# Graph attention on one core: which edge groups make their keys and values from node rows, when, and by what way the rows come

## The chip, the cores and the metric

The kernel runs on one core of a Trainium2 chip. The time is device microseconds of one launch; the figure for the kernel before is the median of three runs. One execution was profiled and gives the trace that is read here. All data start and end in the chip's memory (DRAM below).

## The reference, cut to what matters

There are 3125 nodes with 128 features each (`x`), 100,000 edges sorted by their target `dst`, five relations (`edge_type`), and eight heads of 16 features.

```python
for r in range(5):
    mask = edge_type == r
    q = einsum('eh,khd->ekd', x[dst], W_Q[r])
    k = einsum('eh,khd->ekd', x[src], W_K[r])
    v = einsum('eh,khd->ekd', x[src], W_V[r])
    logits = where(mask, (q * k).sum(-1) / 4 + bias[r], -1e9)
    top = maximum(segment_max(logits, dst), -1e9)
    e = where(mask, exp(logits - top[dst]), 0)
    attn = e / (segment_sum(e, dst)[dst] + 1e-12)
    out += segment_sum(attn[:, :, None] * v, dst)
h = out @ out_w.T + out_b + x
x1 = layernorm(h) * gamma + beta
result = layernorm(x + x1)
```

An edge has one relation, so it needs one key and one value row: those of its source node under its own relation.

## The kernel before, in words

**Table stage (0 to about 110 us).** The nodes are cut into `NT` = 25 blocks of 128. For each block `b`, `turn(b)` transposes the node rows and `table(b)` makes keys and values of all five relations in three fp32 matmuls (L404); ACT and DVE copy them out of PSUM (L408 and beside it) and SP's queue stores 640 KB to `kv_d` in DRAM. Row `node * 5 + relation` of `kv_d` is then 256 fp32: key and value. Beside each block stand jobs of the dictionary `side` (indices, keys and types of the edges are turned and converted), and from `b` = 1 on a gather `in_row` (L435) with an ACT `sign` that counts edges below a node (`count`, L443), eight gathers ahead.

**Loop.** Edges come in `NGR` = 196 groups of 512 (128 partitions x `T` = 4). A hand-written order walks over steps `k`; nothing is rescheduled, so each engine and each queue runs its instructions in the order in which the code issues them. Group `g` has its first half in step `g` and its second half (`v`) 16 to 19 steps later, when the maxima of its node block are there. In a step are issued, in this order:

- SP's queue: `fetch_keys` and `fetch_q` for group `k + 3`, rows of later stages, `fetch_types`, and further down the step `store_logits`.
- POOL: `gather` for group `k + 3`: four indirect DMAs (L699), one for each of the four columns of 128 edges, from `kv_d` into `kvs_[g % 23]`. There are `KVB` = 23 such buffers; the last reader of a buffer is `weigh` (L939). Then, about every eighth step, `maxima_load` (L830, tile `ell`): an indirect DMA that reads back logits stored in the step before.
- ACT: `put_kv` (L791), then `by_node`, `carry` (L988).
- PE: `spread_m` (L921, tile `me`), `sums` (L973, L975, L982), `spread_q` (L804, tile `qe`).
- DVE and ACT: `weigh` (L939), `less_max` (L930), `exps` (L934), `weights` (L947), `norm` (L994), `logits` (L817, L818), `spot` (L795, tile `hot`, made for group `k + 2` and kept in `HELD` buffers until `spread_m` of that group has read it), `places` (L959, L962), and around every eighth step in two steps `maxima` (L868 `wl`, L874 `mx`).
- End of the step: per node block `project`, `roots`, `norms`, and the queries of later blocks (L725).

**The x groups.** For the groups in `XG` (before: 3, 6, 9, 12, 15), `gather` does nothing. Instead the node rows themselves are gathered before the table stage: 20 indirect DMAs (L655) straight into the value half of `kvs_[g]`, with index `src` (tile `xi`), which need no table. Keys and values are then made in the loop, in steps `x_at[g] = step_of[g] - 5` and the two after it:

- `turn_x` (L764): four transposes of the rows into PSUM tile `tx`;
- `by_relation` (L771): for each relation, one DVE instruction that multiplies the rows by `type == r` (tile `xm`, 128 x 2560). `tr` holds the types of the 512 edges on every partition, fetched by `fetch_types` two steps before from `edge_type` as int32 (256 KB);
- `products` (L782), in the step after: twice ten products of 128 x 256, summed over the relations in tile `pk`; an fp32 product has two passes in the trace, so a group has 40;
- `put_kv` (L791), at the head of the step after that: two ACT copies into `kvs_[g]`.

PSUM tiles `tx`, `pk` and `me` carry one tag with two banks: each waits until the reader of the tile before the last is done. `xm` shares its memory with the maxima's `wl` (tag `wl`, one buffer).

Of the kernel before, what the change touches and what calls it, by code (L numbers as in the profile page):

```python
# [8 lines left out]
F32 = mybir.dt.float32  # L9
BF16 = mybir.dt.bfloat16  # L10
I32 = mybir.dt.int32
# [6 lines left out]
P = 128  # L18
# [3 lines left out]
R = 5  # L22
HEADS = 8
HD = 16
H = 128
# [14 lines left out]
GE = 512  # L40
T = GE // P
NGR = -(-E // GE)
HG = 99
HR = NGR - HG
# [14 lines left out]
NSR = E // SR  # L59
SB = P * E // N // SR  # L60
SPAD = 5
XG = range(3, 16, 3)
QB = 3
KVB = 23
HELD = 21
KVA = 9


# [65 lines left out]
def windowed_path(  # L134
# [4 lines left out]
    nc = tc.nc  # L139
# [6 lines left out]
    m_d = dram.tile([NP * R, 3 * HEADS], BF16, name="m_d")  # L146
    lg_d = dram.tile([GP, LW], F32, name="lg_d")
    key_d = dram.tile([NGR, GE], BF16, name="key_d")


    def keep(name, shape, dt=F32):
# [19 lines left out]
    xi = keep("xi", [P, len(XG), T], I32)  # L171

    kvs_ = {}

    def buffers(those):
        for i in those:
# [2 lines left out]
            )  # L179


    at_once = [*(g for g in range(5) if g not in XG), *XG]
    buffers(at_once)
    ahead = ctx.enter_context(tc.tile_pool(name="ahead", bufs=3))

# [7 lines left out]
    xn = load.tile([P, NT, H], F32, name="xn")  # L193
    nc.vector.memset(xn[:, NT - 1, :], 0.0)
    nc.sync.dma_start(xn[:, :4, :], x[: 4 * P].rearrange("(i p) h -> p i h", p=P))
    nc.sync.dma_start(
        xi,
        src[: (NGR - 1) * GE].rearrange("(g p t) -> p g t", p=P, t=T)[
            :, XG.start : XG.stop : XG.step, :
        ],  # L200
    )
    fr = load.tile([1, NGR + NSR], I32, name="fr")
    with nc.allow_non_contiguous_dma(reason="one element of each group"):
        nc.sync.dma_start(
# [257 lines left out]
    def keys_b():  # L462
# [4 lines left out]
        for p0, p1 in ((0, HR - 1), (HR - 1, HR)):  # L467
            nc.scalar.dma_start(
                key_d[HG + p0 : HG + p1, :], keyb[p0:p1, 1].rearrange("g t p -> g (t p)")
            )  # L470

    def keys_c():
        nc.vector.scalar_tensor_tensor(
            kvrow.rearrange("g s i -> g (s i)"), src_r.rearrange("g s i -> g (s i)"), float(R),
            typ_r.rearrange("g s i -> g (s i)"), op0=ALU.mult, op1=ALU.add,
        )
        nc.scalar.activation(typr, typ_r, AF.Identity, bias=1.0)
# [150 lines left out]
    def no_maxima():  # L628
# [18 lines left out]
        13: [lambda: along(typr, 1, put_typ)],  # L647
        14: [no_maxima],
        15: [sorted_rows],
        17: [sorted_ends],  # L650
    }

    for i, g in enumerate(XG):
        for t in range(T):
            nc.gpsimd.indirect_dma_start(  # L655
                out=kvs_[g][:, t, H:], out_offset=None, in_=x[:, :],
                in_offset=bass.IndirectOffsetOnAxis(ap=xi[:, i, t : t + 1], axis=0),
            )
    rows, counted = {}, 0
    xT = {b: turn(b) for b in range(2)}  # L660
    for b in range(NT):
        if b + 2 < NT:
            xT[b + 2] = turn(b + 2)
        table(b, xT.pop(b))
        for f in side.get(b, ()):
            f()
        while b >= 1 and len(rows) < NT and len(rows) - counted < 8:
            rows[len(rows)] = in_row(len(rows))
        if b >= 3:
            count(counted, rows[counted])  # L670
            counted += 1
# [81 lines left out]


    def fetch_types(g):
        tr = ahead.tile([P, GE], I32, name="tr", bufs=1)
        nc.sync.dma_start(tr, edge_type[g * GE : (g + 1) * GE].partition_broadcast(P))
        live["tr", g] = tr

    def turn_x(g):  # L760
        xe = kvs_[g % KVB][:, :, H:]
        tx = ps.tile([P, T, P], F32, name="tx", tag="me")
        for t in range(T):
            nc.tensor.transpose(tx[:, t, :], xe[:, t, :], ident)  # L764
        live["tx", g] = tx

    def by_relation(g):
        tr, tx = live.pop(("tr", g)), live.pop(("tx", g))
        xm = late_flow.tile([P, R, T, P], F32, name="xm", tag="wl", bufs=1)
        for r in range(R):  # L770
            nc.vector.scalar_tensor_tensor(  # L771
                xm[:, r], tr.rearrange("h (p t) -> h t p", t=T), float(r), tx,
                op0=ALU.is_equal, op1=ALU.mult,
            )
        live["xm", g] = xm
# [267 lines left out]
    def norms(b):  # L1043
        sd, mv = live.pop(("sd", b)), live.pop(("mv", b))
        nc.vector.reciprocal(sd, sd)
        if b < NT:
            n = min(P, N - b * P)
            h = live.pop(("h", b))
            nc.vector.scalar_tensor_tensor(
                h[:n], h[:n], mv[:n, 0, 0:1], gamma_t[:n], op0=ALU.subtract, op1=ALU.mult  # L1050
            )
            y = late_flow.tile([P, H], F32, name="y")
            nc.vector.scalar_tensor_tensor(
                y[:n], h[:n], sd[:n, 0:1], live.pop(("xr", b))[:n], op0=ALU.mult, op1=ALU.add
            )
            if ("mv", b + 1) not in live:
                live["mv", b + 1] = pair()
                nc.vector.memset(live["mv", b + 1], 0.0)
            nxt = live["mv", b + 1]
            moments(nxt[:, 1, :], y[:n], n)  # L1060
            live["y", b] = y
        if b:
            n = min(P, N - (b - 1) * P)
            z = late_flow.tile([P, H], F32, name="z")
            nc.vector.tensor_scalar(
                z[:n], live.pop(("y", b - 1))[:n], mv[:n, 1, 0:1], sd[:n, 1:2],
                op0=ALU.subtract, op1=ALU.mult,
            )
            live["z", b - 1] = z
# [36 lines left out]
    norm_at = {b: r + (r < final - 1) for b, r in root_at.items()}  # L1106


    x_at = {g: step_of[g] - 5 for g in XG}
    assert min(x_at.values()) >= -2 and max(x_at.values()) + 2 < at_k[0] - 1  # L1110


    q_from = []
# [10 lines left out]
    for k in range(-4, root_at[NT] + 2):  # L1124
# [20 lines left out]
                fetch_m(u)  # L1145
        for u in XG:
            if x_at[u] - 2 == k:
                fetch_types(u)

        while gathered < NGR - 1 and step_of[gathered + 1] <= k + (AHEAD if k < final - 16 else 1):  # L1150
# [585 lines left out]
```

## Time and profile before

| | |
|---|---|
| runs | 1665.2 us median (1658.07 to 1668.21) |
| profiled execution | time 1665.2 us, span 1663.5 us |
| mean granted TensorE clock | 0.724 |
| busy share of the span | PE 63%, DVE 57%, POOL 48%, ACT 38% |
| table stage, x gathers at the start | L655, 20 gathers from 11.8 us on, 0.944 us each |
| gathers in the loop | L699, 764, 0.948 us each |
| products of the x groups | L782, 200 records, 62.9 us busy |
| masks of the x groups | L771, 25, about 1.055 us each |

The span runs from the first to the last instruction of the profiled execution; the time of a run holds a little more around it. A busy share is the mean over all stages. In the trace PE's matmuls and its weight loads (PEld) are told apart; a "pass" below is one matmul record. Idle time is put down to what released the engine; "issue" is idle time with no such cause in the records.

### The profile page before, as it was taken

The numbers are of one execution on the slowest core, as the hardware profiler recorded it, in microseconds if no ns is written. First come the engines' busy times: TensorE is split into PE (matmuls) and PEld (weight loads), VectorE is DVE, ScalarE is ACT, GpSimd is POOL, SyncE is SP. The second block draws the span as 40 slices with busy tenths as digits, with TensorE's granted clock in tenths as the row PEclk, the third lists the DMA queues.
The fourth block names the chain that finished last, engine by engine and source line by source line (L and its number), as shares of the span: only waits on it lengthen the run. The fifth ranks groups of instructions, "written<-read, shape, count | busy, mean of one in ns | idle before, by whom it ended". The sixth has DMA issues, their size and how long they took to land.

```text
span 1663.5 us, 26129 instructions
## 1 busy us (share of the span) xinstructions
PE 1043.0 (63%) x7746; PEld 790.5 (48%) x7746; DVE 945.4 (57%) x2536; ACT 638.7 (38%) x2258; POOL 796.5 (48%) x901
## 2 busy tenths in 40 slices
PE   6774836356566666665666666666566655665676
PEld 2443624245454444554554554555445544454564
DVE  3452626455564665556466555657555564564686
ACT  1450103144344444434445443444344343334344
POOL 6345061645465545545645554555455455445400
PEclk8885967677676767667676766777666776666878
DMA  6683343445455544544545454555445444444400
GB/s 161 232 309 105 72 134 80 108 124 137 101 135 126 132 110 121 137 109 118 144 118 129 126 137 107 137 131 131 108 120 139 109 122 120 107 118 108 102 16 15
DMA packets 181946, 203.66 MB, mean 122 GB/s; under 512 B 83943, under 2 KB 146819, under 8 KB 181676
## 3 DMA queue, kind: packets, MB, share of 16 engines
q0 software_dynamic: 40576, 112.08, 23.4%
q1 hardware_dynamic: 136790, 85.12, 21.9%
q10 hardware_dynamic: 4430, 4.71, 1.1%
q8 instruction: 64, 1.05, 0.3%
q14 instruction: 86, 0.70, 0.1%
HBM read 166.51 MB, written 35.28 MB: 121 GB/s over the span
## 4 chain that ended last, share of the span: by engine, by line
PE 29%; DVE 28%; issue 19%; another core or an unknown queue 10%; ACT 5%; DMA 2%; SPq 1%; DVEq 0%; ACTq 0%; POOL 0%
PE pp L973 9%; PE qe L804 4%; PE me L921 4%; DVE wl L868 4%; DVE mx L874 4%; DVE prod L817 4%; PE pk L782 3%; DVE wv L939 3%; DVE lg L818 2%; PE pp L975 2%; PE pr L404 2%; ACT at L959 2%; DVE hot L795 2%; PE prq L725 1%
## 5 line engine op out<-in xcount | busy, mean ns | idle before, releaser
L699 POOL DMA_INDIRECT kv<-kv_d,idx x764 | 724.5, 948 | 587.9 <-DVE den L994 346.6
L973 PE MATMUL pp<-wv,at 128*125 128x136 f32 x1568 | 392.7, 385 | 43.3 <-issue 34.1
L973 PEld LDWEIGHTS pp<-wv,at 128*125 128x125 f32 x1568 | 295.7, 256 | 122.4 <-issue 116.0
L804 PE MATMUL qe<-qw,hot 125*128 125x128 bf16 x2352 | 229.9, 256 | 87.7 <-issue 77.6
L921 PE MATMUL me<-mw,hot 125*128 125x64 bf16 (+1 forms) x2352 | 145.3, 217 | 217.6 <-issue 115.2
L804 PEld LDWEIGHTS <-hot 125*128 125x128 bf16 x2352 | 203.3, 125 | 99.6 <-issue 86.3
L921 PEld LDWEIGHTS <-hot 125*128 125x128 bf16 x2352 | 126.6, 113 | 253.5 <-issue 197.0
L934 ACT ACTIVATE me<-me 128x32 f32<-128x32 f32 x196 | 35.7, 182 | 542.0 <-DVE me L930 409.5
L959 ACT ACTIVATE at<-row_at,nkey 128x125 f32<-128x125 f32 x744 | 237.6, 398 | 0.0
L930 DVE TENSOR_TENSOR me<-lg,me 128x32 f32<-128x32 f32 x196 | 37.7, 193 | 348.6 <-remote 195.6
L939 DVE TENSOR_TENSOR wv<-kv,me 128x512 f32<-128x512 f32 x196 | 133.0, 679 | 104.0 <-remote 63.2
L817 DVE TENSOR_TENSOR prod<-kv,qe 128x512 f32<-128x512 f32 x196 | 132.9, 678 | 43.2 <-PE qe L804 25.7
L818 DVE TENSOR_REDUCE lg<-prod 128x32 f32<-128x512 f32 x196 | 134.5, 686 | 6.8
L975 PE MATMUL pp<-pt,carried 125*5 125x136 f32 x390 | 101.4, 350 | 57.8 <-ACT pt L988 27.4
L962 ACT ACTIVATE at<-at 128x500 f32<-128x500 f32 (+1 forms) x196 | 117.3, 599 | 6.2
L725 PE MATMUL prq<-wq,xTq 128*128 128x384 f32 (+1 forms) x88 | 52.7, 693 | 92.9 <-DVE hot L795 61.1
L1007 ACT COPY oT<-pp 128x25 f32 x196 | 33.7, 172 | 180.6 <-PE me L921 72.8
L830 POOL DMA_INDIRECT ell<-lg_d,start_i x25 | 23.6, 944 | 154.3 <-DMA lg_d<-lg 62.0
L782 PE MATMUL pk<-wkv,xm 128*128 128x256 f32 x200 | 62.9, 448 | 50.3 <-issue 46.3
L868 DVE TENSOR_TENSOR wl<-by_head,shut 128x1536 f32<-128x1536 f32 (+2 forms) x49 | 73.1, 1491 | 33.7 <-PE pk L782 25.6
L982 PEld LDWEIGHTS pp<-rsum,o 125*128 125x128 f32 x392 | 83.6, 257 | 14.0 <-issue 13.3
L982 PE MATMUL pp<-rsum,o 125*128 125x25 f32 x392 | 74.2, 270 | 12.8 <-issue 8.2
(191 smaller groups left out, 1199.5 us busy)
## 6 DMA issues: line engine op xcount, KB each, us to landing
kt<-key_d SPq DMA_DIRECT2D x196, 128.0 KB
qw<-q_d SPq DMA_DIRECT2D x196, 96.0 KB
kv_d<-kvs SPq DMA_DIRECT2D x24, 640.0 KB
kv<-kv_d,idx POOLq DMA_INDIRECT x764
q_d<-q SPq DMA_DIRECT2D x22, 480.0 KB
lg_d<-lg SPq DMA_DIRECT2D x196, 18.0 KB
mw<-m_d SPq DMA_DIRECT2D x196, 6.0 KB
xr<-in_x SPq DMA_DIRECT2D x24, 64.0 KB
```

The costliest lines, as they stand in the source:

```text
L699: nc.gpsimd.indirect_dma_start(out=kv[:, t, :], out_offset=None, in_=kv_d[:, :], in_offset=bass.IndirectOffsetOnAxis(ap=idx[:, t, g : g + ...
L804: nc.tensor.matmul(qe[:, t, :], hot[:, t, :], qw[:WR, s, :], start=(s == 0), stop=(s == 2))
L817: nc.vector.tensor_tensor(prod, kv[:, :, :H], live.pop(("qe", g)), op=ALU.mult)
L818: nc.vector.tensor_reduce(lg[:, :, :HEADS], prod.rearrange("p t (k d) -> p t k d", d=HD), AX.X, ALU.add)
L868: nc.vector.tensor_tensor(wl, by_head[:, None].to_broadcast([P, n, nh, D]), shut[:, :n, None, :].to_broadcast([P, n, nh, D]), op=ALU.add,)
L921: nc.tensor.matmul(me[:, t], hot[:, t, :], mw[:WR, None, :, s, :].to_broadcast([WR, times, 2, HEADS // 2]), start=(s == 0), stop=(s == 2),)
L939: nc.vector.tensor_tensor(wv[:, :, :H].rearrange("p t (k d) -> p t k d", d=HD), kv[:, :, H:].rearrange("p t (k d) -> p t k d", d=HD), live ...
L959: nc.scalar.activation(at[:, t, :], row_at[:, :WR], AF.Abs, bias=nkey[:, t, g : g + 1], scale=1.0)
L962: nc.scalar.activation(at[:, on_dve:], at[:, on_dve:], AF.Relu, bias=1.0, scale=-1.0)
L973: nc.tensor.matmul(pp, at[:, t, :], wv[:, t, :], start=(t == 0), stop=(t == T - 1))
L975: nc.tensor.matmul(pp[:R], carried[:WR, g, :], live.pop(("pt", g - 1)), start=False, stop=False,)
L982: nc.tensor.matmul(op, live.pop(("o5", done)), rsum[:WR], start=True, stop=True)
```

## The change

- `XG` becomes 3, 8, 13, 18, 23, 44, 60, 76, 92: nine groups. The loop has 748 gathers (L699) instead of 764.
- The node rows no longer go to the value half of a group's buffer. They are gathered into tile `xs` with four buffers (`XA`): 16 gathers stand at POOL's head before the table stage, and 20 more follow one by one in the iterations `b` = 3 to 22, before that iteration's `count`. `store_x` writes each finished group (256 KB) to `xs_d` in DRAM, on SP's queue, at `b` = 3, 4, 5, 6, 8, 12, 16, 20 and 24. In the loop `fetch_nodes` brings it back into tile `xe` (one buffer).
- The types are converted once to bf16 and put in order (`types_d`, at `b` = 16: one DVE copy and three DMAs issued by ACT) and stored to `typ_d`; `fetch_types` reads 128 KB of bf16 from there, and `by_relation` reads them without a stride.
- `x_at` becomes `step_of[g] - 3`: transposes and masks in step `g - 3`, products in `g - 2`, copies at the head of `g - 1`; both fetches in step `g - 5`.
- `xm` has memory of its own. `HELD` goes from 21 to 20, and `z`, the last result of a node block, has one buffer instead of two.
- The groups whose gathers stand ahead of the loop's other memory (`at_once`) are 0, 1, 2, 4, 5, 6 and 7.

On POOL's queue 11 groups (44 gathers) now stand ahead of the first `ell`, then 7 groups (28) ahead of the second and 7 ahead of the third; before, 9 (36), 8 (32) and 8 (32).

```diff
--- before.py
+++ after.py
@@ -59,10 +59,12 @@
 NSR = E // SR
 SB = P * E // N // SR
 SPAD = 5
-XG = range(3, 16, 3)
+XG = (*range(3, 24, 5), *range(44, 93, 16))
+XE = 5
+XA = 4
 QB = 3
 KVB = 23
-HELD = 21
+HELD = 20
 KVA = 9
 
 
@@ -146,6 +148,8 @@
     m_d = dram.tile([NP * R, 3 * HEADS], BF16, name="m_d")
     lg_d = dram.tile([GP, LW], F32, name="lg_d")
     key_d = dram.tile([NGR, GE], BF16, name="key_d")
+    typ_d = dram.tile([NGR, GE], BF16, name="typ_d")
+    xs_d = dram.tile([len(XG) * P, T * H], F32, name="xs_d")
 
 
     def keep(name, shape, dt=F32):
@@ -179,7 +183,7 @@
             )
 
 
-    at_once = [*(g for g in range(5) if g not in XG), *XG]
+    at_once = [g for g in range(KVA - 1) if g not in XG]
     buffers(at_once)
     ahead = ctx.enter_context(tc.tile_pool(name="ahead", bufs=3))
 
@@ -193,12 +197,9 @@
     xn = load.tile([P, NT, H], F32, name="xn")
     nc.vector.memset(xn[:, NT - 1, :], 0.0)
     nc.sync.dma_start(xn[:, :4, :], x[: 4 * P].rearrange("(i p) h -> p i h", p=P))
-    nc.sync.dma_start(
-        xi,
-        src[: (NGR - 1) * GE].rearrange("(g p t) -> p g t", p=P, t=T)[
-            :, XG.start : XG.stop : XG.step, :
-        ],
-    )
+    by_edge = src[: (NGR - 1) * GE].rearrange("(g p t) -> p g t", p=P, t=T)
+    nc.sync.dma_start(xi[:, :XE, :], by_edge[:, XG[0] : XG[XE - 1] + 1 : XG[1] - XG[0], :])
+    nc.sync.dma_start(xi[:, XE:, :], by_edge[:, XG[XE] : XG[-1] + 1 : XG[-1] - XG[-2], :])
     fr = load.tile([1, NGR + NSR], I32, name="fr")
     with nc.allow_non_contiguous_dma(reason="one element of each group"):
         nc.sync.dma_start(
@@ -469,6 +470,15 @@
                 key_d[HG + p0 : HG + p1, :], keyb[p0:p1, 1].rearrange("g t p -> g (t p)")
             )
 
+    def types_d():
+        typb = load.tile([HG, 2, T, P], BF16, name="typb")
+        nc.vector.tensor_copy(typb, typ_r.rearrange("g s (p t) -> g s t p", t=T))
+        nc.scalar.dma_start(typ_d[:HG, :], typb[:, 0].rearrange("g t p -> g (t p)"))
+        for p0, p1 in ((0, HR - 1), (HR - 1, HR)):
+            nc.scalar.dma_start(
+                typ_d[HG + p0 : HG + p1, :], typb[p0:p1, 1].rearrange("g t p -> g (t p)")
+            )
+
     def keys_c():
         nc.vector.scalar_tensor_tensor(
             kvrow.rearrange("g s i -> g (s i)"), src_r.rearrange("g s i -> g (s i)"), float(R),
@@ -647,15 +657,28 @@
         13: [lambda: along(typr, 1, put_typ)],
         14: [no_maxima],
         15: [sorted_rows],
+        16: [types_d],
         17: [sorted_ends],
     }
 
-    for i, g in enumerate(XG):
+    staged = {}
+
+    def gather_x(i, t):
+        if t == 0:
+            staged[i] = load.tile([P, T, H], F32, name="xs", bufs=XA)
+        nc.gpsimd.indirect_dma_start(
+            out=staged[i][:, t, :], out_offset=None, in_=x[:, :],
+            in_offset=bass.IndirectOffsetOnAxis(ap=xi[:, i, t : t + 1], axis=0),
+        )
+
+    def store_x(i):
+        nc.sync.dma_start(
+            xs_d[i * P : (i + 1) * P, :], staged.pop(i).rearrange("p t h -> p (t h)")
+        )
+
+    for i in range(XA):
         for t in range(T):
-            nc.gpsimd.indirect_dma_start(
-                out=kvs_[g][:, t, H:], out_offset=None, in_=x[:, :],
-                in_offset=bass.IndirectOffsetOnAxis(ap=xi[:, i, t : t + 1], axis=0),
-            )
+            gather_x(i, t)
     rows, counted = {}, 0
     xT = {b: turn(b) for b in range(2)}
     for b in range(NT):
@@ -664,8 +687,13 @@
         table(b, xT.pop(b))
         for f in side.get(b, ()):
             f()
+        for i in range(len(XG)):
+            if b == (i + 3 if i < XA else T * (i - XA + 2)):
+                store_x(i)
         while b >= 1 and len(rows) < NT and len(rows) - counted < 8:
             rows[len(rows)] = in_row(len(rows))
+        if 3 <= b < 3 + T * (len(XG) - XA):
+            gather_x(XA + (b - 3) // T, (b - 3) % T)
         if b >= 3:
             count(counted, rows[counted])
             counted += 1
@@ -753,12 +781,18 @@
 
 
     def fetch_types(g):
-        tr = ahead.tile([P, GE], I32, name="tr", bufs=1)
-        nc.sync.dma_start(tr, edge_type[g * GE : (g + 1) * GE].partition_broadcast(P))
+        tr = ahead.tile([P, GE], BF16, name="tr", bufs=1)
+        nc.sync.dma_start(tr, typ_d[g].partition_broadcast(P))
         live["tr", g] = tr
 
+    def fetch_nodes(g):
+        xe = ahead.tile([P, T, H], F32, name="xe", bufs=1)
+        i = XG.index(g)
+        nc.sync.dma_start(xe.rearrange("p t h -> p (t h)"), xs_d[i * P : (i + 1) * P, :])
+        live["xe", g] = xe
+
     def turn_x(g):
-        xe = kvs_[g % KVB][:, :, H:]
+        xe = live.pop(("xe", g))
         tx = ps.tile([P, T, P], F32, name="tx", tag="me")
         for t in range(T):
             nc.tensor.transpose(tx[:, t, :], xe[:, t, :], ident)
@@ -766,10 +800,10 @@
 
     def by_relation(g):
         tr, tx = live.pop(("tr", g)), live.pop(("tx", g))
-        xm = late_flow.tile([P, R, T, P], F32, name="xm", tag="wl", bufs=1)
+        xm = late_flow.tile([P, R, T, P], F32, name="xm", bufs=1)
         for r in range(R):
             nc.vector.scalar_tensor_tensor(
-                xm[:, r], tr.rearrange("h (p t) -> h t p", t=T), float(r), tx,
+                xm[:, r], tr.rearrange("h (t p) -> h t p", p=P), float(r), tx,
                 op0=ALU.is_equal, op1=ALU.mult,
             )
         live["xm", g] = xm
@@ -1061,7 +1095,7 @@
             live["y", b] = y
         if b:
             n = min(P, N - (b - 1) * P)
-            z = late_flow.tile([P, H], F32, name="z")
+            z = late_flow.tile([P, H], F32, name="z", bufs=1)
             nc.vector.tensor_scalar(
                 z[:n], live.pop(("y", b - 1))[:n], mv[:n, 1, 0:1], sd[:n, 1:2],
                 op0=ALU.subtract, op1=ALU.mult,
@@ -1106,8 +1140,8 @@
     norm_at = {b: r + (r < final - 1) for b, r in root_at.items()}
 
 
-    x_at = {g: step_of[g] - 5 for g in XG}
-    assert min(x_at.values()) >= -2 and max(x_at.values()) + 2 < at_k[0] - 1
+    x_at = {g: step_of[g] - 3 for g in XG}
+    assert min(x_at.values()) >= -2
 
 
     q_from = []
@@ -1145,6 +1179,7 @@
                 fetch_m(u)
         for u in XG:
             if x_at[u] - 2 == k:
+                fetch_nodes(u)
                 fetch_types(u)
 
         while gathered < NGR - 1 and step_of[gathered + 1] <= k + (AHEAD if k < final - 16 else 1):
```

## The prediction

> **What bounds the kernel now.** I read the page first, then the waits, the windows by stage, and the timeline inside the gather bursts.
>
> From the page (busy time and count of each engine; then slices of the span; then the chain that ended last; then groups: operands and count, busy, mean ns, idle before and its releaser):
>
> ```profile
> span 1663.5 us, 26129 instructions
> PE 1043.0 (63%) x7746; PEld 790.5 (48%) x7746; DVE 945.4 (57%) x2536; ACT 638.7 (38%) x2258; POOL 796.5 (48%) x901
> ...
> PEclk8885967677676767667676766777666776666878
> ...
> PE 29%; DVE 28%; issue 19%; another core or an unknown queue 10%; ACT 5%; DMA 2%; SPq 1%; DVEq 0%; ACTq 0%; POOL 0%
> ...
> L699 POOL DMA_INDIRECT kv<-kv_d,idx x764 | 724.5, 948 | 587.9 <-DVE den L994 346.6
> ...
> L782 PE MATMUL pk<-wkv,xm 128*128 128x256 f32 x200 | 62.9, 448 | 50.3 <-issue 46.3
> ```
>
> No engine is full; the chain changes between PE and DVE, and "issue" has a fifth of it. The stages:
>
> ```profile
> core 0: us, PE busy (x) PEld busy (x) DVE busy (x) ACT busy (x) POOL busy (x), PEclk, DMA share, GB/s
> ...
> 60.00:108.00 48.00, 47.50 (x162) 26.78 (x162) 25.67 (x50) 30.63 (x85) 14.74 (x16) 1.00 0.88 336
> 108.00:147.00 39.00, 19.36 (x70) 13.38 (x70) 14.67 (x44) 6.03 (x20) 27.01 (x29) 0.64 0.57 172
> 147.00:284.00 137.00, 81.72 (x502) 59.99 (x502) 64.28 (x113) 21.02 (x69) 38.72 (x41) 0.75 0.35 88
> 284.00:336.00 52.00, 23.49 (x189) 17.99 (x188) 23.53 (x60) 12.26 (x48) 31.33 (x33) 0.65 0.46 118
> 336.00:1507.00 1171.00, 735.40 (x5864) 577.36 (x5862) 694.19 (x1877) 493.71 (x1760) 614.24 (x648) 0.71 0.49 123
> ```
>
> The table loop (60 to 108) is PE-bound: 47.5 us of 48. The long middle, 1171 us for 161 steps (7.3 us each), has PE, DVE and POOL at 63, 59 and 52%: a chain in order, not one full engine. Two stalls stand out in the start of the loop:
>
> ```profile
> POOL kv L699 <- issue: 203.0, 661, 1.0
> ...
> POOL ell L830 <- ACT kv L791: 48.5, 1, 48.5
> ```
>
> A gather occupies POOL 0.948 us and the next issues 0.30 later: 1.25 us each, 5.0 per group. What a long burst of them does to the others is in the timeline, 24 us into a burst:
>
> ```profile
> 135.45 0.38 PE L782 MATMUL pk<-wkv,xm 128*128 128x256 f32 x1 [1.60 <-issue]
> 137.55 0.59 PE L782 MATMUL pk<-wkv,xm 128*128 128x256 f32 x1 [1.73 <-issue]
> ```
>
> One pass per some 2 us, with nothing to wait for, where 32 such passes take 7.17 us (0.224 each) outside. I call it the crawl: from about 10 us into a back-to-back burst all engines together issue 2 to 3 instructions per us until it ends (36–52, 134–157, 234–250 and 290–318 us). In the last-but-one the maxima of the first node block stood behind the products, in the timeline of DVE:
>
> ```profile
> 254.99 1.76 DVE L868 TENSOR_TENSOR wl<-by_head,shut 128x1536 f32<-128x1536 f32 x1 [25.58 <-PE pk L782]
> ```
>
> **The parts and their prices.** The sum is made against the profiled execution: span 1663.5, time 1665.2 (1.7 around the span), which is also the median shown.
>
> *Table stage.* The 20 gathers of x rows at the start become 16; 20 more follow one by one in iterations 3 to 22. Before, 20 + 8 gathers ran back to back (11.8 to 47.4) and PE stood in the crawl between 36 and 52 with gaps of 4.45 and 6.80 us and smaller ones; up to 13 us can be won, since the first 16 end at 31.8. Against this, an iteration of 2.15–2.26 us has one gather now and gets two: 2 × 1.25 = 2.5 us of POOL, up to 2.9 with POOL's wait for `sign`. So 19 iterations pay 0.25 to 0.65: +5 to +12. The DMA engines also get 20 × 64 KB and some 9 × 256 KB in this stage, 3.6 MB on the 16.1 MB that 336 GB/s × 48 us moved: share 0.88 × 1.22 = 1.08, +4 if they bind. That is parallel to the POOL term, not on top. I take −13 + 7 = −6 (bounds −13 and +8). The type conversion (a DVE copy, three DMAs issued by ACT) lies in iteration 16, where DVE and ACT are busy 54 and 64% behind PE: nothing; without that cover under 3 us.
>
> The Trainium skill, "DMA: Bandwidth & Descriptors", section Bandwidth, puts the ceiling of a core's DMA engines at about 435 GB/s; as an estimate from that page, 410 GB/s would still fit and the loop pay nothing, while the row's share makes full load 336/0.88 = 382 GB/s and the loop pay 4. No run here shows the ceiling.
>
> *Loop start up to the first `ell`.* POOL runs 11 groups (44 gathers) instead of 9 (36) before it: +10, in the crawl. The steps ahead of it hold the x work of groups 3 and 8 instead of 3, 6, 9 and 12. An x group there costs 9.7 us (14.5 us per cycle of three steps, 4.8 of them plain), but group 3 falls into the burst in both and part of 13 comes early: −14. Net −4, bounds −9 (two full groups, −19.4) and +5.
>
> *Second burst.* 28 gathers instead of 32: −5. Maxima have their own `wl` now: the 25.6 us wait is gone, but PE is in the crawl there anyway, so only DVE's 3.5 us after it are saved. Group 18 comes in, +9.7; with what part of 13 is left, +11. Net +2.5, bounds −9 and +12. Then 28 instead of 32 again, and group 23: −5 + 9.7 = +4.7, bounds −5 and +10.
>
> *Groups 44, 60, 76, 92.* Each removes 4 gathers and adds, over steps g−3 to g−1, 4 transposes and 40 passes on PE, five mask products on DVE and two copies on ACT, ahead of `by_node` and `exps` on ACT, so exps wait with them. The mask products read int32 types with a stride before:
>
> ```profile
> L771 DVE SCALAR_TENSOR_TENSOR xm<-tr,tx x25: 1040/1055/1089, 124.9 to 226.0; 128x512 f32<-128x512 int32 x25
> ```
>
> Five took 4.95 us. With bf16 in order I take 0.68 each, the row of `prod` with the same 512 elements: 3.4 (bounds 2.7 and 5.0). Start times of the step's multiply (L817) give the mean step by place in the block of eight: 7.1, 6.6, 6.8, 10.7, 7.4, 7.0, 5.6, 7.5, sum 58.7. x falls on places 1 to 3: mean 23.4 us together, with 12 gathers and one `ell`, 16.25 us of POOL. After: POOL has 11.25, and PE's queue has a chain, because `tx`, `pk`, `pk` and `me` share two PSUM banks: DVE 4.5 + 3.4 (its own work, then the masks), `me`, sums and `qe` 2.9, then pass block 4.5, copy 0.9, pass block 4.5, copy 0.9, then the rest 2.6: 24.2. So +1 each, +4 for four. Bounds each: −2.7 (four gathers less, 5.0; 110 instructions more at the 48 per us of gather-free steps, 2.3) and +6.
>
> The passes are counted at full clock; windows with bursts were granted 0.64. The Trainium skill's "TensorE: Matmul & The Clock Gate", section "What's actually happening", says that an idle window of about 3.4 us halves the clock and one busy window restores it. The masks' 3.4 us would be such a gap; as an estimate from the page, 7.6 passes go at half rate and a group costs 10.7 instead of 9.0, +1.7, so +7 in four. The row nearest, 224 ns in a dense block of 32, gives none. I leave it out of the sum.
>
> *Hidden edits.* HELD 20: `spot` (L795) must wait for the `me` matmuls of its own step; but `less_max` (L930), ahead of it on DVE, waits for the same matmuls, so nothing (if that cover were gone, up to 12 × 0.217 = 2.6 us of `me` (row of L921) per step). `xe` (256 KB) and types (128 KB instead of 256) are fetched two steps early, some 14 us, on SP's queue ahead of that step's logits store; type rows landed 2.7 to 4.9 us after issue even in bursts: nothing.
>
> *Tail.* One buffer for z: six stores in a row each wait for the one before, and z starts now stand 4.3, 1.7, 1.7, 3.2 and 0.6 us apart against some 2.3 of landing: +2 (0 to +4).
>
> Sum: −6 − 4 + 2.5 + 4.7 + 4 + 2 = +3.2, so 1665.2 + 3.2 = **1668.4 us**: no change that could be told. A measurement of this kernel tells a change of about 1% from none, here 16.7 us.
>
> **Rivals.**
> *Gathers are the price of a step (faster).* For it: position means contain 16.25 us of POOL in 23.4, gather-free steps run in 2.3 to 3.3 us (L817 at 274.2, 276.8, 279.9), and the crawl says that gathers slow everyone. Then table stage −8, first part −9, second −3, third 0 (x hidden behind shorter bursts), four groups −2.7 × 4 = −10.8, tail +2: −29, upper end; half of the doubtful early terms gives −22: **1643**. Against it: POOL is 52% busy in the middle, and its largest wait, 346.6 us, is for DVE's `den` (L994), so gathers there often have slack.
>
> *Cold passes (slower).* Steps g−2 of the four late groups: PE stands while DVE makes masks, then runs 40 passes at the clock of burst windows, 0.65: 40 × 0.224/0.65 = 13.8 instead of 9.0, +4.8 each, +19: **1687**. The same row of passes has mean 448 ns against 376 minimum, so part of them is slow already. It decides when a late group costs more than 4.4 us (1 + 13.5/4); against it, PE becomes denser there, and dense stretches (60 to 108) are granted 1.00.
>
> *The rows are not there (slower).* `tx` stands in PE's order, so a late `xe` stops PE: its 256 KB come back through queues whose share is 0.49. If it landed 5 us after the turn was due in the six groups from 18 on: +30, **1698**. Against it: 14 us of lead.
>
> **How the numbers follow.** My forecast 0.45 (itself 0.03 faster, 0.40 same, 0.02 slower; its own range 1650 to 1682), gathers 0.30 (all faster), cold passes 0.20, late rows 0.05. So faster 0.33, same 0.40, slower 0.27. The range reaches from the faster rival to past the cold one: 1640 to 1695; the bounds of the terms make no more than that likely.
>
> **What would show it.** The table loop's iterations at 2.4 to 2.6 us and no PE gaps near 36–52; the first `ell` around 195 rather than 205.2; no 25.6 us wait at L868; masks near 0.68 us each; blocks of eight with x about 59.7 against 58.7; `tx` waiting for a DMA nowhere. It is wrong if blocks with x are under 56 or over 63 us, if the iterations exceed 2.9, or if the start-up ends more than 15 us off.

## The result, and the profile after

The changed kernel takes 1705.5 us (median of 4 runs) against 1663.7 of the kernel before: 1.0259 times the time, 95% interval 1.0219 to 1.0299. The forecast was 1668.4 and no change, range 1640 to 1695; it was slower and past the range. The profiled execution has a span of 1708.9 us against 1663.5, so 45.4 us are to be found (it is the slowest of the four, 5 us above their median). From its page:

```profile
span 1708.9 us, 26522 instructions
PE 1057.8 (62%) x7922; PEld 810.7 (47%) x7922; DVE 948.7 (56%) x2557; ACT 645.8 (38%) x2266; POOL 800.1 (47%) x901
...
PE 30%; DVE 26%; another core or an unknown queue 17%; issue 15%; ACT 7%; DMA 2%; SPq 1%; DVEq 0%; POOL 0%; ACTq 0%; POOLq 0%
...
L727 POOL DMA_INDIRECT kv<-kv_d,idx x748 | 710.1, 949 | 631.9 <-DVE den L1028 372.8
...
L816 PE MATMUL pk<-wkv,xm 128*128 128x256 f32 x360 | 96.7, 433 | 53.8 <-DVE xm L805 36.0
```

The groups do what the change says: 748 gathers, 360 passes. PE is 15 us busier (the passes went from 62.9 to 96.7, the rest shrank by 19), and no share rose. The loss is in waiting: POOL's gathers stand idle 631.9 us instead of 587.9. The same stages as before:

```profile
core 0: us, PE busy (x) PEld busy (x) DVE busy (x) ACT busy (x) POOL busy (x), PEclk, DMA share, GB/s
...
60.00:108.00 48.00, 33.49 (x100) 16.46 (x100) 15.94 (x33) 20.02 (x57) 31.11 (x32) 0.93 0.80 287
108.00:147.00 39.00, 17.30 (x83) 12.60 (x81) 13.27 (x44) 10.94 (x36) 21.68 (x23) 0.65 0.67 213
147.00:284.00 137.00, 66.35 (x385) 53.29 (x386) 50.50 (x96) 14.69 (x46) 47.91 (x51) 0.68 0.38 98
...
336.00:1507.00 1171.00, 747.50 (x5951) 587.36 (x5952) 684.80 (x1840) 485.72 (x1716) 584.26 (x616) 0.73 0.47 120
```

In 60 to 108 PE was full before (47.5 us) and is busy 33.5 now. Where the time went, from the start times of gathers and of the step's multiply (before L817, now L851), in us, after minus before: first gather of the loop +7.1 (111.5 to 118.6); first `ell` +10.5 (205.2 to 215.7); second +6.2; third +13.6; step 40 +10.2; step 104 +49.8; last multiply +44.3; end +45.4. So 10 us were lost by step 40, 39.6 in steps 40 to 104, where the four late groups are (44, 60, 76 and 92; the five others are called early), and the rest of the loop gave 5.5 back.

Group 60 on PE, with start, duration and the idle time before:

```profile
594.67 0.61 PE L798 MATMUL tx<-ident,xe 128*128 128x128 f32 x4
600.98 0.82 PE L955 MATMUL me<-mw,hot 125*128 125x64 bf16 x12 [5.70 <-DVE xm L805]
...
605.14 4.54 PE L816 MATMUL pk<-wkv,xm 128*128 128x256 f32 x20
613.88 6.27 PE L816 MATMUL pk<-wkv,xm 128*128 128x256 f32 x20 [4.21 <-ACT kv L825]
620.83 0.52 PE L955 MATMUL me<-mw,hot 125*128 125x64 bf16 x12 [0.68 <-ACT kv L825]
```

The second half of the products waits for the first ACT copy, and `me` of the next step waits for the second. DVE and POOL stand meanwhile:

```profile
621.45 0.20 DVE L964 TENSOR_TENSOR me<-lg,me 128x32 f32<-128x32 f32 x1 [16.16 <-PE me L955]
```

The masks before it and the first copy, on DVE and ACT, and the end of POOL's burst of gathers:

```profile
597.84 3.08 DVE L805 SCALAR_TENSOR_TENSOR xm<-tr,tx 128x512 f32<-128x512 bf16 x5 [3.71 <-remote]
613.24 0.59 ACT L825 COPY kv<-pk 128x512 f32<-128x512 f32 x1 [7.33 <-remote]
```

```profile
610.55 0.95 POOL L727 DMA_INDIRECT kv<-kv_d,idx  x1 [0.30 <-issue]
626.21 0.94 POOL L727 DMA_INDIRECT kv<-kv_d,idx  x1 [14.71 <-DVE den L1028]
```

From the end of the masks (600.9) to `me` of the next step (620.8) are 19.9 us; in the four groups 22.2, 19.9, 19.9 and 21.3. The prediction had 13.7 for this piece.

### The profile page after: what moved, and what is told of

The parts are those of the page before. It is cut to its first block, busy times and chain, and to the rows that moved or that the text cites. A ratio compares the mean times of both kernels' runs of the same rounds, so it can differ in the third digit from the quotient of the medians.

```text
span 1708.9 us, 26522 instructions
## 1 busy us (share of the span) xinstructions
PE 1057.8 (62%) x7922; PEld 810.7 (47%) x7922; DVE 948.7 (56%) x2557; ACT 645.8 (38%) x2266; POOL 800.1 (47%) x901
## 4 chain that ended last, share of the span: by engine, by line
PE 30%; DVE 26%; another core or an unknown queue 17%; issue 15%; ACT 7%; DMA 2%; SPq 1%; DVEq 0%; POOL 0%; ACTq 0%; POOLq 0%
PE pp L1007 8%; PE me L955 4%; PE pk L816 4%; DVE wl L902 4%; DVE mx L908 4%; PE qe L838 3%; DVE prod L851 3%; PE pr L405 3%; DVE wv L973 2%; DVE lg L852 2%; ACT at L993 2%; PE pp L1009 2%; DVE hot L829 1%; PE prq L753 1%
## 5 line engine op out<-in xcount | busy, mean ns | idle before, releaser
L727 POOL DMA_INDIRECT kv<-kv_d,idx x748 | 710.1, 949 | 631.9 <-DVE den L1028 372.8
L1007 PE MATMUL pp<-wv,at 128*125 128x136 f32 x1568 | 384.3, 378 | 35.8 <-issue 27.7
L1007 PEld LDWEIGHTS pp<-wv,at 128*125 128x125 f32 x1568 | 286.5, 249 | 119.5 <-issue 116.6
L955 PE MATMUL me<-mw,hot 125*128 125x64 bf16 (+1 forms) x2352 | 138.8, 213 | 219.5 <-issue 92.2
L838 PEld LDWEIGHTS <-hot 125*128 125x128 bf16 x2352 | 202.2, 125 | 109.8 <-issue 92.5
L955 PEld LDWEIGHTS <-hot 125*128 125x128 bf16 x2352 | 120.6, 111 | 252.6 <-issue 157.8
L851 DVE TENSOR_TENSOR prod<-kv,qe 128x512 f32<-128x512 f32 x196 | 132.9, 678 | 41.4 <-ACT kv L825 24.9
L816 PE MATMUL pk<-wkv,xm 128*128 128x256 f32 x360 | 96.7, 433 | 53.8 <-DVE xm L805 36.0
L816 PEld LDWEIGHTS pk<-wkv,xm 128*128 128x128 f32 x360 | 77.8, 221 | 70.1 <-DVE xm L805 36.3
```

What stands on the lines that cost most here:

```text
L727: nc.gpsimd.indirect_dma_start(out=kv[:, t, :], out_offset=None, in_=kv_d[:, :], in_offset=bass.IndirectOffsetOnAxis(ap=idx[:, t, g : g + ...
L816: nc.tensor.matmul(pk[:, t, :], xm[:, r, t0 + t, :], wkv[:, r].rearrange("h s c -> h (s c)"), start=(r == 0), stop=(r == R - 1),)
L838: nc.tensor.matmul(qe[:, t, :], hot[:, t, :], qw[:WR, s, :], start=(s == 0), stop=(s == 2))
L851: nc.vector.tensor_tensor(prod, kv[:, :, :H], live.pop(("qe", g)), op=ALU.mult)
L955: nc.tensor.matmul(me[:, t], hot[:, t, :], mw[:WR, None, :, s, :].to_broadcast([WR, times, 2, HEADS // 2]), start=(s == 0), stop=(s == 2),)
L1007: nc.tensor.matmul(pp, at[:, t, :], wv[:, t, :], start=(t == 0), stop=(t == T - 1))
```

## The experiments

Runs fell on chips of two kinds. On the first (both kernels above, and f1 to f3) the kernel before takes 1664 to 1670 us in the median and the engines crawl in gather bursts. On the second it takes 1215 to 1223 us and they don't. Each ratio below is to the kernel before on the same chip. The price of a late group is taken from the traces: the time from step 40 to step 104, less that of the kernel before on the same kind of chip (460.9 us on the first, 335.2 on the second), over four. It is one execution each. On the second kind six executions without late groups lie within 4.7 us in this stretch, so a price is good to about 1 us. On the first it is less sure: from step 104 to the last multiply, where their instructions are the same, the changed kernel and f1 to f3 took 2 to 11 us less than the kernel before, which would be up to some 3 us of price. Each diff below shows the deciding lines alone.

| kernel | chip | ratio (95%) | price of a late group |
|---|---|---|---|
| changed | first | 1.0259 (1.0219 to 1.0299) | 9.9 |
| a0_after, the same | second | 1.0446 (1.0398 to 1.0494) | 12.6 |
| e1_early | second | 0.9979 (0.9953 to 1.0005) | (none left) |
| e2_late | second | 1.0377 (1.0335 to 1.0420) | 12.0 |
| e3_bank | second | 1.0386 (1.0347 to 1.0424) | 11.2 |
| e4_nogather | second | 1.0389 (1.0341 to 1.0438) | |
| e7_split | second | 1.0313 (1.0263 to 1.0363) | 10.5 |
| e8_quarter | second | 1.0289 (1.0238 to 1.0341) | 7.6 |
| e6_own | second | 0.9986 (0.9957 to 1.0015) | |
| e11_early_split | second | 0.9881 (0.9845 to 0.9918) | (none left) |
| f1_noprod | first | 1.0006 (0.9961 to 1.0051) | 1.2 |
| f2_nomask | first | 1.0125 (1.0036 to 1.0214) | 2.8 |
| f3_quarter | first | 1.0170 (1.0083 to 1.0257) | 4.2 |

### Which groups lose the time

```diff
 e1_early
-XG = (*range(3, 24, 5), *range(44, 93, 16))
+XG = tuple(range(3, 24, 5))
 e2_late
+XG = tuple(range(44, 93, 16))
```

> Only the five early groups (3, 8, 13, 18, 23) are left; 44, 60, 76 and 92 are plain gathers again. Theory A (each late group stops the loop: xm, two banks, copies held back; some 8 us each, 31 to 35 us in all between steps 40 and 106): 1670 to 1676 us. Rival B (the table stage and the start of the loop lost it, and the late blocks would make it good): about 1695 us. If A holds, a start of the loop near +12 against before stays in the trace.

> Only the four late groups (44, 60, 76, 92); the early ones are plain gathers, so the first burst has 12 groups, and nothing is gathered between table blocks. Theory A: the late loss of 31 to 35 us stays, steps 40 to 106; the start is 5 to 15 us better than in the changed kernel because the table loop is free: 1690 to 1700 us. Rival B (the early x groups pay for themselves, since gathers are what the start is made of): the start gets worse by 10 or more, 1715 us or above.

The times that were expected belong to the first kind of chip; the ratios can be read. Without the late groups nothing is lost, 0.998; with them alone most of the loss is there, 1.038 against the 1.0446 of a0_after on another chip. The early groups as the change places them are worth nothing on this kind of chip, neither way: at step 40 the traces read 318.1 (e1_early) and 323.0 (e2_late) against 326.9 of the kernel before, a few us of 1220. Both ran once more on another chip of the second kind:

> e1_early once more (early groups 3, 8, 13, 18 and 23 alone). On a chip with the crawl: steps 40 to 106 lose nothing, the start loses less than the 13 us of the changed kernel, since 4 gathers instead of 20 stand between table blocks: 1.000 to 1.006 of the kernel before. Rival (the start's loss is that of the early groups themselves): 1.007 to 1.012. On a chip without: 0.998 as before.

> e2_late once more (groups 44, 60, 76 and 92 alone). On a chip with the crawl: 40 us from the late groups, as in the first comparison, and a first burst of 48 gathers against chains of x groups that are gone: 1.015 to 1.030. On a chip without: 1.038 as before.

0.9982 (0.9948 to 1.0016) and 1.035 (1.031 to 1.039): the same.

### The two kinds of chip

> The kernel before, unchanged, to have its profile beside the experiments: the chip of the first experiments ran it in 1214.9 us, not 1663.7. If the difference is the crawl in gather bursts (no engine but POOL issues after some 10 us), this profile shows matmuls at full rate inside the first burst, few waits of POOL, and 1210 to 1220 us; if it is something else (slower gathers, a lower clock), bursts look alike and single instructions differ in length.

> The changed kernel, unchanged, beside the kernel before on the chip of the experiments. If the loss is made by the four late groups, as e2_late suggests (ratio 1.038), it is again 1.036 to 1.042 of the kernel before. If a good part of the first comparison's loss came from the start and table stage, where a chip without the crawl loses nothing, it is below 1.02.

The kernel before had 1223.6 us here. In its first burst the products run at full rate while POOL gathers, on PE and on POOL:

```profile
131.56 7.17 PE L782 MATMUL pk<-wkv,xm 128*128 128x256 f32 x32 [0.27 <-DVE xm L771]
```

```profile
126.83 0.94 POOL L699 DMA_INDIRECT kv<-kv_d,idx  x1 [0.30 <-issue]
```

A gather's median is 946 ns on both kinds, so the gathers are not faster; the others are not held up by them. Why one kind crawls was not found out. The changed kernel loses more here, 1.0446, so a loss of this size does not need the crawl; what the crawl adds on the first kind is a separate question, taken up further down. The piece from the masks to `me`, in a0_after:

```profile
431.43 4.54 PE L816 MATMUL pk<-wkv,xm 128*128 128x256 f32 x20
436.64 4.58 PE L816 MATMUL pk<-wkv,xm 128*128 128x256 f32 x20 [0.68 <-ACT kv L825]
441.90 0.52 PE L955 MATMUL me<-mw,hot 125*128 125x64 bf16 x12 [0.67 <-ACT kv L825]
```

Here ACT copies as soon as the first half ends, while POOL is in a burst of eight gathers:

```profile
436.01 0.59 ACT L825 COPY kv<-pk 128x512 f32<-128x512 f32 x1 [3.93 <-PE pk L816]
```

```profile
436.12 0.95 POOL L727 DMA_INDIRECT kv<-kv_d,idx  x1 [0.30 <-issue]
```

The piece takes 14.8 to 15.7 us in the four groups, near the 13.7 that were predicted, and DVE still stands for it (10.95 us in this group). Yet the price is 12.6. The three steps that hold a late group's work, from the multiply of step g-3 to that of step g, take 25.9 us on average, near the predicted 24.2; but in b0_before the same steps take 13.3, not 23.4. Here the chain comes on top of the block.

### Is it the PSUM banks, the place, or the work

```diff
 e3_bank
-        pk = ps.tile([P, 2, KVW], F32, name="pk", tag="me")
+        pk = ps.tile([P, 2, KVW], F32, name="pk", tag="me" if t0 else "fin", bufs=2 if t0 else 1)
 e7_split (x_at one step earlier)
             if x_at[u] + 1 == k:
                 products(u, 0)
+            if x_at[u] + 2 == k:
                 products(u, 2)
 e8_quarter (products and copies follow pieces)
-    x_at = {g: step_of[g] - 3 for g in XG}
+    x_at = {g: step_of[g] - (6 if g > 40 else 3) for g in XG}
+    pieces = {g: T if g > 40 else 2 for g in XG}
```

> The first half of the products goes to the bank of tag fin, so the second half need not wait for the first ACT copy, and the matmuls of me wait for one copy only. Theory A1 (the chain through two PSUM banks makes the late groups dear): the 4.2 us gap of PE between the halves goes and the second half runs at full clock, 6 to 7 us less per late group, 1678 to 1685 us. Rival A2 (the added PE, DVE and ACT work itself lengthens an ordered chain, whichever bank it uses): no more than 2 us per group, 1698 to 1706 us.

> The products of an x group are spread over two steps (half in each), and all of it starts one step earlier. Theory A2 (PE's order: DVE waits 12.4 us for me while both halves run, since nothing else of PE may pass them): the wait is cut in two, and each half hides partly behind a step's DVE work; a late group costs 6 to 8 us instead of 12, 1.020 to 1.028 of the kernel before. Rival A3 (the sum of PE's work counts, wherever it is put): 12 us as it was, 1.036 to 1.042. Rival A1 (two PSUM banks) is taken for fallen by e3_bank.

> The products of the four late groups are spread over four steps (ten passes each), starting three steps earlier; early groups as in the changed kernel. Theory A2: PE is 2.3 us longer in each of four steps, most of it hidden; a late group costs 0 to 4 us, 1.00 to 1.014 of the kernel before. Rival A3: 1.03 or more. A third outcome, that ACT waits longer because copies into the group's buffer now come when its last reader has just begun, would show as waits of ACT at the copies and 1.02 to 1.03.

e3_bank takes the wait between the halves away (in its trace the second half follows the first at once), and the price falls only from 12.6 to 11.2: on this kind of chip the banks are a small part. But PE's wait between the halves is 0.68 us here against 4.2 on the first kind, where this edit was not run; what it would save there is not shown. Two halves in two steps: 10.5, between what the two theories gave. Its 17 us on the changed kernel come mostly from the start: step 40 at 310.0 instead of 322.8, the largest piece between steps 20 and 24, where group 23 is (25.4 us instead of 34.9). Quarters in four steps: 7.6. In e8_quarter a late group's first copies come ahead of the last read of the group 23 earlier, so part of that group's values differ. In the late groups ACT's copies wait for nothing but the passes; it is `weigh` of the old group that waits for the copy, 2.7 to 4.0 us in three of the four late groups, 10.2 in all. Up to 2.6 of the 7.6 can come from that order, so the quarters themselves cost some 5 to 7.6. So spreading helps a little with each cut, and on this kind of chip none of the cuts hides all of the work.

### How much room POOL's gathers leave

```diff
 e9_plain1 (in the kernel before) and e10_x1 (in the changed one)
-        for t in range(T):
+        for t in range(T if g < KVB else 1):
```

> The kernel before with one gather instead of four for each group from 23 on (three quarters of its keys and values stay from 23 groups earlier): POOL has 9 instead of 33 gathers in a block of eight steps and can bound nothing. It shows how long the ordered chain of the other engines is. Theory A3 (engines are in balance, the chain of a plain block is nearly as long as POOL's 41.3 us): blocks of 37 to 41 us, 1130 to 1200 us in all. Rival A2 (the chain has much room under POOL): blocks under 34 us, below 1080 us. On a chip with the crawl: far under 1663, since bursts are gone.

> The same cut in the changed kernel (one gather per group from 23 on). Theory A3: the blocks with x are longer than the plain ones of e9_plain1 by the time for which PE does nothing else, 10 to 14 us each, and the end is 40 to 55 us later than there, as with all gathers: POOL has no part in the price of an x group. Rival A4 (the price comes from POOL standing still and not catching up): less than 6 us each, under 25 us in all.

e9_plain1 leaves out 519 of 764 gathers, and takes 1167.8 us against the 1222.5 of the kernel before: 55 us for 649 us of gathers at 1.25 each, 0.1 us per gather. The line of busy times of e9_plain1, then of e10_x1:

```profile
PE 851.3 (73%) x7746; PEld 662.9 (57%) x7746; DVE 940.3 (81%) x2536; ACT 637.6 (55%) x2258; POOL 304.6 (26%) x382
```

```profile
PE 892.8 (73%) x7922; PEld 701.0 (57%) x7922; DVE 944.9 (77%) x2557; ACT 641.7 (52%) x2266; POOL 321.3 (26%) x397
```

With POOL at 26% the blocks of eight steps from 32 to 104 still take 37.7 to 40.2 us, against POOL's 33 x 1.25 = 41.3 with all gathers and 40.3 to 43.2 measured in b0_before. So the ordered chain of PE, DVE and ACT is nearly as long as POOL's list, and taking 5 us from POOL can give back some 1 to 3 (an estimate from these blocks). With the same cut the changed kernel is 56.5 us slower (1224.3), 14.7 per late group between steps 40 and 104: POOL has no part in the price there. This decides, on the second kind and with one execution each, for the chain and against POOL standing still and failing to catch up. On the first kind neither edit was run.

### What the price is made of, on the first kind of chip

```diff
 f1_noprod
-            if x_at[u] + 1 == k:        (products; likewise + 2, the copies)
+            if x_at[u] + 1 == k and u < 40:
 f2_nomask
-        for r in range(R):
+        for r in range(R if g < 40 else 1):
 f3_quarter (e8_quarter, one step later)
-    x_at = {g: step_of[g] - (6 if g > 40 else 3) for g in XG}
+    x_at = {g: step_of[g] - (5 if g > 40 else 3) for g in XG}
```

> The changed kernel with the products and the two copies of groups 44, 60, 76 and 92 left out (these groups keep the keys and values of the groups before in their buffers); rows, types, transposes and masks are still made. Theory A3 (nothing hides work that is put into the ordered chain): the passes with their two copies, 11 us of each late group, go; 44 us less than the changed kernel's 1.0446, so 1.005 to 1.012 of the kernel before. Rival (masks, fetches, banks and transposes have half of the price): 1.02 or more.

> The changed kernel with one mask instead of five for the four late groups (relations 1 to 4 multiply what the group before left in xm). Theory A3: 4 x 0.6 = 2.4 us of DVE less per late group, all of it on the chain, 10 us in all: 1.034 to 1.040 of the kernel before. Rival (the masks are hidden, PE has slack there): 1.041 to 1.048. It can only just be told.

> e8_quarter with the late groups one step later, so that each copy follows the last read of the buffer. e8_quarter was 1.0289 and its blocks of 16 steps were 7.6 us longer than plain ones. If the order of the buffer had no part in that: 1.024 to 1.034. If ACT's copies waited there: 1.015 to 1.022.

Without passes and copies the late groups cost 1.2 us instead of 9.9 and the kernel is level with the one before: rows, transposes and masks alone cost little, the price comes with the passes and their copies. f3_quarter: 4.2 instead of 9.9, where e8_quarter had 7.6 instead of 12.6. It differs from e8_quarter in the step and in the kind of chip, so which of the two made the difference is not shown. f2_nomask missed: 2.4 us less of DVE took 7 us off. The three steps of a late group went from 33.8 to 28.4 us on average. Of these 5.4 us the masks are 2.4, and the piece from the masks to `me` gives 2.3 (18.5 instead of 20.8): in groups 44 and 92 ACT's first copy follows the passes at once (4.76 and 4.58 us for the halves of 44), in 60 and 76 it is held back by 2.5 and 2.9 us. Why it is held in two groups and not in the others was not settled. The traces also overstate these gains: the profiled execution of the changed kernel is the slowest of its four, those of f2 and f3 are the fastest of theirs. By the ratios f1, f2 and f3 save 10.5, 5.6 and 3.7 us per late group, by the traces 8.7, 7.1 and 5.7.

### Table stage, own memory, and a version that beats both

```diff
 e4_nogather (store_x writes one of the first four groups again)
-        if 3 <= b < 3 + T * (len(XG) - XA):
-            gather_x(XA + (b - 3) // T, (b - 3) % T)
 e6_own (in the kernel before; HELD 20, one buffer of z)
-        xm = late_flow.tile([P, R, T, P], F32, name="xm", tag="wl", bufs=1)
+        xm = late_flow.tile([P, R, T, P], F32, name="xm", bufs=1)
```

> The 20 gathers of node rows among the table blocks are left out; groups 23 to 92 get the rows of groups 3 to 18 instead, so their values are not the reference's; the stores to DRAM stay. Theory C (POOL, with two gathers per block and in bursts, sets the pace of the table stage): the last table block is issued 6 to 13 us earlier than at 111.1 us, 1693 to 1699 us. Rival D (the stores on SP's queue and the full DMA engines set it): the table stage ends within 2 us of before this edit, 1704 to 1707 us.

> The kernel before with own memory for xm (20 buffers of hot and one of z make room). As predicted: the maxima of the first block do not wait for the products, 3.5 us less, and the tail costs 2 us more: 0.995 to 1.001 of the kernel before. In the traces of this chip that wait was 5.1 us rather than 25.6, so little can be seen.

> Only the five early groups of the changed kernel, their products spread over two steps as in e7_split: the parts that the runs favour. e7_split was 13 us ahead of the changed kernel at step 40, and e1_early had 0.998 of the kernel before. If the early gain stands by itself: 0.982 to 0.992 of the kernel before. If it was of that run only: 0.995 to 1.001.

The last table block is issued at 87.1 us in e4_nogather, 87.5 in a0_after and 89.6 in the kernel before on such a chip: there the 20 gathers don't pace the table stage, and theory C falls for it. The stores don't either: with five of them in e1_early the last table block comes at 88.5 us, with four in e2_late at 88.7, with nine in a0_after at 87.5. On the first kind it wasn't tried. e6_own is level, 0.9986: the 3.5 us and the 2 us of the prediction can't be told apart. e11_early_split (five early groups, products over two steps, and one buffer less in a late stage to make room) is faster than both kernels: 0.9881. Once more on another chip of the second kind:

> e11_early_split once more. On a chip with the crawl: the early products stand in the bursts, where splitting them gains little: 0.994 to 1.004 of the kernel before. On a chip without: 0.988 as before.

0.9879 (0.9856 to 0.9901). On the first kind of chip it was not measured.

## Why the prediction was wrong, point by point

**Groups 44, 60, 76 and 92, +1 each: this step failed.** Measured 9.9 each; the blocks of eight with x took 65.1 to 67.5 us, above the 63 at which the prediction called itself wrong. The step put a chain of 24.2 us in place of 23.4 measured for three steps. The 23.4 holds: the twelve steps took 23.5 per group in the kernel before (the list of places next to it adds up to 24.1). In the changed kernel they took 33.8. So on this kind of chip it was the chain that was sized wrong, by 9.6 us.

The mis-sized term is masks to `me` of the next step: 13.7 predicted, 20.8 measured on average, 7.1 of the 9.6. Piece by piece in group 60: `me`, sums and `qe` 4.2 instead of 2.9; first half 4.5 as predicted; copy 4.2 with its wait instead of 0.9; second half 6.3 instead of 4.5; copy 0.7 instead of 0.9. The copy was ready to go at 609.7 by the passes and ran at 613.24, after POOL's last gather of the burst (610.55 + 0.95). In all four groups it was held back, by 3.1 to 3.8 us, and ran 1.7 to 2.0 us after that gather's end; in a0_after it ran 0.04 us after the passes in all four, in group 60 with POOL in the same kind of burst. The prediction knew the crawl and did not put ACT's copy into it. What holds the copy is not known, so that the burst does it is read from the traces and was not tested by a run.

PE's gap then cost the clock: in group 60 seven of the 20 passes of the second half came 0.43 us apart instead of 0.22, and two lay between. The Trainium skill's "TensorE: Matmul & The Clock Gate", section "What's actually happening", was cited for the gap behind the masks, with an estimate of +1.7 per group, and left out of the sum. In group 60 the `me` matmuls behind that gap are slow (0.82 us against 0.52 later) and the first half is at full rate; it is the gap between the halves that costs: 6.27 against 4.54 in groups 60 and 76, +1.7, and more in the two others (6.82 and 7.58). In a0_after, where the gap is 0.68 us, the second half takes 4.58. So the half rate after a gap agrees with the page, and the gap stood in another place than the prediction had thought.

The other 2.5 us lie outside that term. A part is the start of the masks: in group 60 the transposes end at 595.3 and the masks begin at 597.84, 1.1 us after a burst's last gather; in a0_after they begin 0.5 us after the transposes. The masks themselves were 0.68 us each as taken:

```profile
L805 DVE SCALAR_TENSOR_TENSOR xm<-tr,tx x45: 677/682/689, 179.1 to 848.0; 128x512 f32<-128x512 bf16 x45
```

On the second kind of chip the same step fails in another place. The chain has nearly its predicted length there (25.9 for 24.2), but the three steps that it replaces take 13.3 us, and 11.1 with a quarter of the gathers in e9_plain1: little of them hangs on the gathers, and the price is 12.6. How much of the 23.5 us of the first kind hangs on the gathers was not tried, and stays open. The rival "gathers are the price of a step" falls on the second kind by e9_plain1, and on the first by the result alone, which went the other way. The rival "cold passes" named the right place and direction, and 1687 us was nearer than the forecast, but with the wrong share: at full clock, on the second kind, the price is no smaller.

**Table stage, -6: wrong, +7.1.** The first half held: the fifth table block came 11 us earlier (54.0 to 43.0). Then POOL ran two gathers per block almost without a pause, and the table loop slowed: 3.4 us per block on average (43.0 to 111.1 over 20), where 2.5 to 2.9 were allowed for. That this is the crawl, now in the table loop itself, is argued from the second kind and was not tested by a run. One such stop on PE:

```profile
70.95 4.50 PE L405 MATMUL pr<-wkv,xT 128*128 128x512 f32 x6 [4.93 <-DVE kvs L411]
```

The same start in f1 to f3 lost 2.5 to 5.4 us, so the sign stands and the size scatters. On the second kind the blocks come 2.8 us apart (a0_after), and the stage loses nothing. There it reached 351 GB/s at a share of 0.96 (57 to 104 us), so full load would be some 366 GB/s, an estimate from this row. That is nearer to the prediction's 382 from the trace than to the 435 that it took from the Trainium skill's "DMA: Bandwidth & Descriptors", section Bandwidth.

**Loop start.** To the first `ell` +3.4 (predicted -4, inside its bounds), second burst -4.3 (+2.5, inside), third +7.4 (+4.7, inside). The signs of two were wrong; that the sum comes near (+6.5 against +3.2) is luck.

**Hidden edits and tail.** `tx` waited for no row of `xe` in the late groups, so the rival of the late rows falls, and the L868 wait of 25.6 us is gone (the line is L902 now), as said. The tail has +1.1 us from the last multiply to the end, against +2.

## What to carry to other kernels

Before work is moved from an engine that looks like the limit, cut that engine's work away and see how long the rest of the chain is: here, on the quick kind of chip, three quarters of the gathers gave 55 us of 1222, so four groups' worth could give 2. Work that is put into an ordered chain can cost nearly its full length (12.6 us there, for some 13 of passes, masks and copies), and less when it is cut small enough to fill the gaps that are there. And a small copy on an engine with little to do is dear when the bottleneck's order waits for it: on the slow kind 0.6 us of copy held PE for 4.2.

## What the runs showed of the hardware that was not expected

Chips differ: the same kernel took 1215 to 1223 us on some and 1664 to 1670 on others, with gathers of the same length (median 946 ns); the mean granted clock was 0.81 on the quick kind and 0.72 on the slow. On the slow kind a long burst of indirect DMAs leaves the other engines almost without instructions. It sets in after no fixed time: in the kernel before, the rate at which they start instructions falls some 22, 9 and 5 us into the first three bursts of the loop (at 134, 214 and 290 us). In the changed kernel's first burst (118.6 to 173.8 us) the transposes for the masks ended at 135.1 us, DVE passed its wait for the types at 141.4 and began the masks at 179.1; SP issued nothing between 146.9 and 171.4. What holds the engines there is not known.
